# A fused attention, state-space and expert kernel: the order of work in its end phase

## The chip, the core and the metric

The kernel runs on one core of a Trainium2 chip. A core has five engines that each run their own list of instructions in order and wait for each other by semaphores: TensorE (PE in the profile; PEld is its weight load), VectorE (DVE), ScalarE (ACT), GpSimd (POOL) and SyncE (SP), which here issues the loads and stores. The metric is the time of one execution on the device in microseconds (us). Lower is better.

## What is computed

One layer in three parts, for 16 sequences of 128 rows and 512 columns, all in float32:

```python
x = x + xattn(layernorm(x), ctx, ...)   # 16 heads, 2048 context rows a sequence
x = x + mamba_mlp(layernorm(x), ...)
x = x + ffn(layernorm(x), ...)

def mamba_mlp(Z):                       # 1024 channels, 16 states
    x, z = split(Z @ in_proj.T)
    x = silu(causal_conv(x) + conv_b)
    dt, Bm, Cm = split(x @ x_proj.T)    # "B and C projection"
    dt = softplus(dt @ dt_proj.T + dt_b)
    h[t] = exp(dt * A) * h[t-1] + dt * Bm * x   # the scan; y[t] = sum(h * Cm)
    y = ((y + x * D) * silu(z)) @ out_proj.T
    Zm = rmsnorm(y + Z)
    return rmsnorm(gelu(Zm @ w1.T + b1) @ w2.T + b2 + Zm)

def ffn(x):                             # gates from softmax(x @ W_gate), best two
    return x @ W_shared.T + (w1 + w2) * (x @ W_expert.T) + bias
```

The expert routing of the reference has one weight matrix for all experts, and every token keeps both of its places, so its sum is the second matrix times the two gates' sum.

## The kernel before, in words

**Steps.** The whole program is one loop over steps `u` (L1275), written out by hand for all engines. In steps 0 to 255 each step does one head group of the attention for one block of 512 context rows. The state-space part runs behind it: sequences are taken in groups `g` of two, and the 32 scan steps of a group start 54 steps behind its first one (32 for the attention of two sequences and `LAG` = 22). A step does two scans: for each, ACT writes the decays exp(dt A) into a PSUM tile (`decays`, L668), DVE scans over it (`scan`, L683) with inputs that POOL made a step before (`inputs`, L646), multiplies by C and clears the first column again, and POOL adds the product up. `bc` tiles hold B and C spread over all partitions; SP loads them from a small DRAM tensor `bcd`, two steps and one step ahead (`load_bc`, L595).

**Late work.** Tables written ahead of the loop name what else a step does: `late` functions (each with a PSUM bank), `behind`, `middle`, `between`, `after`, `inner` and `loads`. For group g with p = 32(g+1): `x_part` and `z_part` (input projection) in steps p+9 to p+16, `silu_first` a step behind each, `silu_third` on ACT and POOL in the step after that; `x_proj` (L582), the B and C projection, at p+18: 16 matmuls over the eight channel blocks, a DVE copy into the single tile `xd`, a store to `bcd`. `dt_first` (L616) multiplies `xd` again, at p+19 for the first block (L1190), in the table `behind`, which comes after `late` in the step. `projected` (L711), the output projection, follows the last scan of a group: for the last one in steps 311 and 313.

**The end phase.** From step 257 on the attention is over, the last group's scans still run to step 309, and the MLP and expert work of all 16 sequences is fed in. It is cut into pairs `m` of two sequences (0 to 7) and into units (`unit`, L1065): a list of loads, of PE work, and of work behind it (`post`). `feed(k)` (L1102) issues the loads of unit k+2, the extra loads of unit k+1, the post work of unit k-1, then the PE work of unit k. The loop feeds 65 units in 57 steps (L1293), so that eight steps take two; the rest follows behind the loop. For a pair the units are:

- `hidden` 0 to 3 (h0 to h3): 32 matmul instructions each into two banks. Behind each: `gelus`, a load of the GELU table, four GELUs, a load of the table with exp and ln.
- `experts` 0 and 1 (e0, e1), of the pair before: first and second matrix and the gate, 16 + 8 + 16 instructions, one sequence each. Behind them `result`, `gated`, `result_last` and the store of the output.
- `second` 0 to 3 (s0 to s3): 16 instructions each, adding into two banks over all four. Behind s1: `z_norm` of the next pair; s2 ends with `turned_in` of the next pair (transposes), behind it come `turned_pair` (copies to SBUF) and `with_b2`; behind s3: `mlp_sum`.

Of the pair before, `mlp_norm` (behind h0), `last_norm` (behind h1) and `x_turned` (transposes of xf and DVE copies fT, ahead of h3) prepare the experts. The last pair has a unit of its own for `turned_in`, directly behind s3 of pair 6.

**Norm factors.** `inv_sqrt` (L93) has three parts: `root_first`, one DVE add (rv); `root_second`, Ln and Exp on ACT (ry, L83 and L84); `root_third`, a Newton step on DVE (rt and the factor, L89 to L91). `mlp_sum`, `mlp_norm` and `z_norm` call it whole, directly behind the moments.

**Order within a step** (L1275 on): loads, `decays` for the first scan, the feeds, `load_bc` for C, `inputs` of the next step, `silu_third`, the first scan, `decays` for the second, the second scan, `middle`, `late`, `behind`, `after`, `inner`, `silu_second`.

**Banks.** In the end phase six PSUM banks are handed out first in, first out (`bank`, `give_back`, L761): a bank given back in program order may be taken at once, and its next writer then waits for its last reader.

Of the kernel before, what the change touches and what calls it, by code (L numbers as in the profile page):

```python
# [27 lines left out]
MB = 2  # L28
# [6 lines left out]
def perceiver_layer(ctx: ExitStack, tc: tile.TileContext, a: dict, out: bass.AP):  # L35
# [40 lines left out]
    def root_first(pool, src, eps):  # L76
        n = src.shape[1]
        v, y, t = (pool.tile([P, MB], FP, tag=k, name=k)[:, 0:n] for k in ("rv", "ry", "rt"))
        nc.vector.tensor_scalar_add(v, src, eps)
        return v, y, t  # L80

    def root_second(v, y, t):
        nc.scalar.activation(y, v, AF.Ln)  # L83
        nc.scalar.activation(y, y, AF.Exp, scale=-0.5)  # L84

    def root_third(dst, v, y, t):
        for j in range(v.shape[1]):
            dj, vj, yj, tj = (x[:, j : j + 1] for x in (dst, v, y, t))
            nc.vector.tensor_scalar(tj, yj, yj, vj, ALU.mult, ALU.mult)  # L89
            nc.vector.tensor_scalar(tj, tj, -0.5, 1.5, ALU.mult, ALU.add)  # L90
            nc.vector.tensor_scalar(dj, yj, tj, None, ALU.mult)  # L91

    def inv_sqrt(pool, dst, src, eps):  # L93
        r = root_first(pool, src, eps)
        root_second(*r)
        root_third(dst, *r)
# [12 lines left out]
    with ExitStack() as es:  # L109
# [472 lines left out]
        def x_proj(g, ps):  # L582
            ps = ps[:, 0:GT]
            for ec in range(EC):
                nc.tensor.matmul(
                    ps,
                    xproj[:, ec * NX : ec * NX + P],
                    xas[g, ec],
                    start=(ec == 0),
                    stop=(ec == EC - 1),  # L590
                )
            nc.vector.tensor_copy(xd[0:NX, :], ps[0:NX, :])
            nc.sync.dma_start(bcd[g], xd[DTR:NX, :])

        def load_bc(t, base):  # L595

            if 0 <= t < 32 * NG:
                g, q = t // 32, t % 4
                x = ssm.tile([P, NH, GT], FP, tag=f"bc{base}", name=f"bc{t}_{base}")
                rows = bcd[g][base + q * NH : base + (q + 1) * NH, :]  # L600
                nc.sync.dma_start(
                    x.rearrange("p n t -> p (n t)"),
                    rows.rearrange("n t -> (n t)").partition_broadcast(P),
                )
                bcs[t, base] = x
# [348 lines left out]
        def mlp_sum(m, ii):  # L954

            n = len(ii)
            mv2, r, ms = small("mv2", [P, n, 2]), small("r2", [P, n]), small("ms", [P, n])
            for j, i in enumerate(ii):
                x = xrs[m * MB + i]
                nc.vector.tensor_tensor(x, x, accs[m][i], ALU.add)  # L960
                give_back(accs[m][i])
                moments(keep, mv2[:, j, :], x)
            mean_square(keep, ms, mv2)
            inv_sqrt(keep, r, ms, 1e-6)
            stage[m, *ii, "r2"] = r

        def mlp_norm(m, ii):

            n, r = len(ii), stage.pop((m, *ii, "r2"))
            mv3, r3 = small("mv3", [P, n, 2]), small("r3", [P, n])  # L970
            for j, i in enumerate(ii):
                b = m * MB + i
                x = xrs[b]
                nc.vector.scalar_tensor_tensor(
                    x, x, r[:, j : j + 1], fcs["normw"], ALU.mult, ALU.mult
                )
                nc.vector.tensor_tensor(x, x, stage.pop((b, "x1")), ALU.add)
                moments(keep, mv3[:, j, :], x)
            inv_sqrt(keep, r3, mv3[:, :, 1], 1e-5)
            stage[m, *ii, "r3"] = mv3, r3  # L980

        def flat_tile(name):
            return fpool[0].tile([P, D], FP, tag="xf", name=name, bufs=4)

        def last_norm(m, ii):
            mv3, r3 = stage.pop((m, *ii, "r3"))
            for j, i in enumerate(ii):
                b = m * MB + i
                xf = flat_tile(f"xf{b}")
                nc.vector.tensor_scalar(  # L990
                    xf, xrs[b], mv3[:, j, 0:1], r3[:, j : j + 1], ALU.subtract, ALU.mult
                )
                nc.gpsimd.tensor_tensor(xrs[b], xrs[b], fcs["fbias"], ALU.add)
                stage[b, "xf"] = xf

        def gated(m, ii):

# [62 lines left out]

        units = []

        def unit(loads=(), pe=(), post=()):  # L1065
            units.append(([*loads], [*pe], [*post], []))
# [1 line left out]
        def call(f, *xs):  # L1068
            return lambda: f(*xs)

        def turn_unit(m, loads):
            unit(
                loads,
                [call(z_norm, m)] + [lambda i=i, b=b: turned_in(xrs[b], b, "mT") for i, b in seqs(m)],
                [call(turned_pair, m)],
            )

        both = tuple(range(MB))
# [1 line left out]
        def hidden_units(m):  # L1080
            for q in range(0 if m else 2, 4):
                unit([call(load_wf, m, 1, q)], [call(hidden, m, q)], [call(gelus, m, q)])
            if m:
                units[-4][2].append(call(mlp_norm, m - 1, both))
                units[-3][2].append(call(last_norm, m - 1, both))
                units[-1][1].insert(0, call(x_turned, m - 1, both))

        def expert_units(m):
            for i in both:
                unit((), [call(experts, m, both, i)], [call(result, m, i)])  # L1090
            units[-1][2].append(call(gated, m, both))
            units[-1][2].extend(call(result_last, m, i) for i in both)

        def second_units(m):
            for q in range(4):
                unit([call(load_wf, m, 2, q)], [call(second, m, q)])
            units[-4][3].append(call(load_x1, m))
            units[-2][2].append(call(with_b2, m))
            if m < NF - 1:
                units[-1][2].append(call(mlp_sum, m, both))  # L1100

        def feed(k):  # L1102
            for f in (units[k + 2][0] if k + 2 < len(units) else ()):
# [9 lines left out]

        for m in range(NF - 1):
            hidden_units(m)
            if m:
                expert_units(m - 1)
            second_units(m)
            if m < NF - 2:
                units[-4][3].append(call(load_z, m + 1))  # L1120
                units[-3][2].append(call(z_norm, m + 1))
                units[-2][1].extend(
                    lambda i=i, b=b: turned_in(xrs[b], b, "mT") for i, b in seqs(m + 1)
                )
                units[-2][2].append(call(turned_pair, m + 1))
        units[0][0].clear()
        units[1][0].clear()
        feeds = len(units) - 1
# [4 lines left out]
        hidden_units(m)  # L1133
        second_units(m)
        for i in both:
            units[-1][1].extend(call(f, m, (i,)) for f in (mlp_sum, mlp_norm, last_norm))
        expert_units(m - 1)
        units[-1][1].insert(0, call(x_turned, m, (0,)))
        units[-1][1].append(call(x_turned, m, (1,)))
# [11 lines left out]
        def put(where, u, f):  # L1151
            where.setdefault(u, []).append(f)
# [24 lines left out]
        for g in range(NG):  # L1177
            p = 32 * (g + 1)
            for ec in range(EC):
                put(loads, p + 8 + ec, lambda g=g, ec=ec: load_win(g, ec))  # L1180
                put(loads, p + 8 + ec, lambda g=g, ec=ec: load_win(g, EC + ec))
                put(late, p + 9 + ec, lambda ps, g=g, ec=ec: x_part(g, ec, ps))
                put(late, p + 9 + ec, lambda ps, g=g, ec=ec: z_part(g, ec, ps))
                put(after, p + 10 + ec, lambda g=g, ec=ec: silu_first(g, ec, xas))
                put(after, p + Z_GATES[ec], lambda g=g, ec=ec: silu_first(g, ec, zss))
            put(late, p + 18, lambda ps, g=g: x_proj(g, ps))
            s = p + LAG
            for ec in range(EC):
                put(loads, s - 4 + 4 * ec, lambda ec=ec: load_dtproj(ec))
                put(behind, s - 3 + 4 * ec, lambda ps, g=g, ec=ec: dt_first(g, ec, ps))  # L1190
                put(middle, s - 2 + 4 * ec, lambda g=g, ec=ec: dt_second(g, ec))
                put(between, s - 1 + 4 * ec, lambda g=g, ec=ec: dt_third(g, ec))
            for i in range(GB):
                for ec in range(WS):
                    put(loads, s + 32 + 2 * i, lambda g=g, i=i, ec=ec: load_wout(g, i, ec))
                put(loads, s + 31 + 2 * i, lambda b=g * GB + i: reload_x(b))
                put(late, s + 33 + 2 * i, lambda ps, g=g, i=i: projected(g, i, ps))
# [77 lines left out]
        for u in range(last):  # L1275
# [11 lines left out]
                load_ctx(made + 1, ("c01",))  # L1287
            for f in loads.get(u, ()):
                f()
            if scans:  # L1290
                decays(g, r, 0)
            if u > NU:
                while fed < feeds * (u - NU) // (last - 1 - NU):  # L1293
                    feed(fed)
                    fed += 1
            load_bc(u + 1 - 32 - LAG, DS)
            if u == NU + 1:
                load_rows()
# [160 lines left out]
```

## Time and profile before

| what | us |
|---|---|
| median of 3 runs | 3772.5 (3771.56 to 3773.25) |
| the profiled execution | 3772.78 |
| its span, first to last instruction | 3771.0 |

| stretch (us) | PE | DVE | ACT | POOL busy |
|---|---|---|---|---|
| 3094 to 3629: end phase up to the first `projected` of the last group | 514.4 of 535 | 408.0 | 276.2 | 376.8 |
| 3629 to 3771: behind it | 132.4 of 142 | 47.4 | 21.1 | 7.7 |

Matmuls are pipelined, so that a busy PE is not PE at its peak: instructions of 512 columns take 592 ns each in the profile, and 16 of them take 6.9 us. In a line of the waits stand the engine, the tile and line that waited, who released it, the total in us, the times and the longest. In a line of the timeline stand start, length, engine, line, operation, tiles, shape and count; in square brackets the idle time before it and who ended that. "issue" is time for which the profile shows no releaser.

### The profile page before, as it was taken

To read this page: it belongs to the slowest core of one execution; us is meant where nothing else is said; L and a number is where in the kernel's file an instruction comes from. 1 tells how busy PE (TensorE), PEld (TensorE's weight loads), DVE (VectorE), ACT (ScalarE), POOL (GpSimd) and SP (SyncE) were. 2 spreads that over 40 slices of the span, in tenths; PEclk is the share of its full clock that TensorE was granted. 3 is DMA by queue.
4 is the path that set the end of the run, shared out by engine and by line. 5 is a ranking of instruction groups with operands and counts; after the bars stand their busy time and mean duration, and the time that the engine had idled before them with its cause. 6 is when DMAs were issued, how large, how long until landed. Compare 5 with 4: busy or idle time off the path is not lost.

```text
span 3771.0 us, 70359 instructions
## 1 busy us (share of the span) xinstructions
PE 3725.5 (99%) x26120; PEld 2853.4 (76%) x26120; DVE 2705.0 (72%) x4854; ACT 2443.5 (65%) x5848; POOL 2111.2 (56%) x1969
## 2 busy tenths in 40 slices
PE   9999999999999999999999999999999999999999
PEld 7878787778777887788788878787878776655555
DVE  3444445887878777877788778877887777778843
ACT  4555556777767776777677767776777775545431
POOL 2111213675767666766676566766675667677720
PEclk9999999999999999999999999999999999999999
DMA  3111122344444435353534353445344458577742
GB/s 102 35 40 43 51 70 80 132 151 144 144 161 143 155 114 186 130 166 115 187 132 147 125 193 119 155 129 181 137 155 135 163 192 283 188 277 249 266 169 73
DMA packets 343226, 548.42 MB, mean 145 GB/s; under 512 B 24369, under 2 KB 227409, under 8 KB 342625
## 3 DMA queue, kind: packets, MB, share of 16 engines
q1 hardware_dynamic: 342432, 543.27, 43.5%
q8 instruction: 206, 3.38, 0.4%
q14 instruction: 140, 1.14, 0.1%
q0 software_dynamic: 448, 0.63, 0.1%
HBM read 527.29 MB, written 16.52 MB: 144 GB/s over the span
## 4 chain that ended last, share of the span: by engine, by line
PE 91%; DVE 5%; ACT 1%; DMA 1%; issue 1%; POOL 1%; SPq 0%; DVEq 0%; ACTq 0%; POOLq 0%
PE pa L240 24%; PE pc L240 17%; PE bank L333 12%; PE bank L302 7%; PE avp L346 7%; PE bank L531 5%; PE bank L1037 2%; PE bank L942 2%; PE bank L472 2%; PE bank L716 2%; PE bank L911 1%; PE avp L399 1%; PE pc L716 1%; PE pa L942 1%; PE avp L942 1%
## 5 line engine op out<-in xcount | busy, mean ns | idle before, releaser
L310 DVE TENSOR_REDUCE nm<-bank 128x1 f32<-128x512 f32 x1024 | 635.2, 682 | 224.0 <-PE bank L302 223.8
L703 POOL TENSOR_TENSOR ysum<-ysum,w 128x512 f32<-128x512 f32 x384 | 500.3, 1303 | 474.8 <-DVE hst L666 306.8
L320 ACT ACTIVATE pr<-bank,nm 128x512 f32<-128x512 f32 x1024 | 689.8, 687 | 89.9 <-DVE nm L310 84.5
L652 POOL TENSOR_TENSOR w<-dx,bc 128x512 f32<-128x512 f32 x512 | 654.2, 1298 | 8.7
L687 DVE TENSOR_TENSOR_SCAN hst<-hst,w 128x512 f32<-128x512 f32 x459 | 560.7, 1221 | 14.3 <-ACT hst L673 8.1
L338 ACT COPY pT<-bank 128x512 f32<-128x512 f32 x816 | 433.9, 585 | 177.6 <-PE bank L333 173.5
L673 ACT ACTIVATE hst<-dt,alog 128x254 f32<-128x254 f32 x918 | 439.5, 479 | 150.4 <-DVE hst L666 130.7
L333 PE MATMUL bank<-ident,pr 128*128 128x128 f32 x4096 | 507.8, 273 | 3.3 <-ACT pr L320 2.8
L333 PEld LDWEIGHTS bank<-ident,pr 128*128 128x128 f32 x4096 | 467.9, 141 | 47.2 <-issue 11.1
L346 PEld LDWEIGHTS avp<-pT,v 128*32 128x32 f32 x8192 | 208.0, 109 | 193.8 <-issue 176.0
L690 DVE TENSOR_TENSOR w<-hst,bc 128x512 f32<-128x512 f32 x459 | 317.3, 691 | 27.6 <-DMA bc<-bcd 12.0
L232 POOL TENSOR_TENSOR t<-c,c 128x512 f32<-128x512 f32 x128 | 163.2, 1275 | 256.6 <-PE pc L240 252.4
L302 PE MATMUL bank<-kt,qT 32*128 32x512 f32 x2048 | 295.4, 640 | 0.5 <-ACT pT L338 0.5
L346 PE MATMUL avp<-pT,v 128*32 128x128 f32 x8192 | 276.7, 276 | 0.0
L240 PE MATMUL pa<-t,ks 128*128 128x256 f32 x1024 | 248.6, 386 | 0.0
L240 PE MATMUL pa<-vs,t 128*128 128x256 f32 x1008 | 244.7, 386 | 0.0
L240 PEld LDWEIGHTS pa<-vs,t 128*128 128x128 f32 x1008 | 185.4, 190 | 34.6 <-issue 10.1
L240 PEld LDWEIGHTS pa<-t,ks 128*128 128x128 f32 x1024 | 184.8, 190 | 35.2 <-issue 11.6
L320 ACT ACTIVATION_READ_ACCUMULATOR pr<-bank,nm 128x1 f32 x1024 | 210.0, 205 | 0.0
L336 DVE COPY pT<-bank 128x512 f32<-128x512 f32 x208 | 143.8, 691 | 87.5 <-PE bank L333 86.2
L232 POOL TENSOR_TENSOR t<-c,t 128x512 f32<-128x512 f32 x128 | 163.8, 1279 | 36.2 <-issue 19.2
L531 PE MATMUL bank<-zT,win 128*128 128x256 f32 x800 | 183.1, 379 | 0.0
(323 smaller groups left out, 6901.1 us busy)
## 6 DMA issues: line engine op xcount, KB each, us to landing
bc<-bcd SPq DMA_DIRECT2D x512, 512.0 KB, 4.3
c<-in_ctxT_dram SPq DMA_DIRECT2D x256, 256.0 KB, 4.4
wf<-in_w_dram SPq DMA_DIRECT2D x124, 512.0 KB, 6.8
wqo<-in_wqkvo_dram SPq DMA_DIRECT2D x128, 256.0 KB, 4.8
win<-in_win_dram SPq DMA_DIRECT2D x128, 256.0 KB, 4.4
wout<-in_wout_dram SPq DMA_DIRECT2D x128, 256.0 KB, 4.4
x<-in_x_dram SPq DMA_DIRECT2D x16, 256.0 KB, 4.0
x1d<-x SPq DMA_DIRECT2D x16, 256.0 KB, 2.1
```

Of the source, the lines that this page charges most:

```text
L240: nc.tensor.matmul(ps[:, r, :], l[:, kc, r * P : (r + 1) * P], m[:, kc, :], start=(i in (1, 2, 5) and r == 0 and kc == 0), stop=(r == 1 an ...
L302: nc.tensor.matmul(banks[j], qts[b][rows, hg, :], kts[u // 4, hg][rows, :], start=True, stop=True)
L310: nc.vector.tensor_reduce(stats[b][0][j][:, sb, hg : hg + 1], banks[j], AX.X, ALU.max, negate=True)
L320: nc.scalar.activation(pr[:, j, :], banks[j], AF.Exp, bias=nm[j][:, sb, hg : hg + 1], accum_out=sm[:, sb, h : h + 1],)
L333: nc.tensor.transpose(ps[:, j, :], prs[u][:, j, i * P : (i + 1) * P], ident)
L338: nc.scalar.copy(pT, ps)
L346: nc.tensor.matmul(avp[j * HD : (j + 1) * HD, hg, :], vts[u // 4, hg // 2, i // 2][:, i % 2, hg % 2 * P + j * HD : hg % 2 * P + (j + 1) * HD],
L531: nc.tensor.matmul(ps, w[:, kc, :], zTs[g][:, kc, :], start=(kc == 0), stop=(kc == KC - 1))
L652: nc.gpsimd.tensor_tensor(w, dx.unsqueeze(1).to_broadcast([P, NH // 2, GT]), bcs[g * 32 + r, 0][:, i * NH // 2 : (i + 1) * NH // 2, :], AL ...
L673: nc.scalar.activation(bt(h[:, k, :])[:, :, 1:], bt(dt)[:, :, 1:], AF.Exp, scale=aneg[:, ec, n : n + 1],)
L687: nc.vector.tensor_tensor_scan(flat, flat, w.rearrange("p n t -> p (n t)"), 0.0, ALU.mult, ALU.add)
L703: nc.gpsimd.tensor_tensor(s, s, w, ALU.add)
```

## The change

It changes the order alone; every matmul, norm and copy is still done.

- `expert_units(m - 1)` is called behind `second_units(m)` and no longer ahead of it. In the new order a pair's units are h0 to h3, s0 to s3, then e0, e1 of the pair before.
- `x_turned` of the pair before goes from the front of h3 to the front of s2. `fbias` is added in a function of its own, `with_bias`, behind h2; for the last pair it stays directly behind `last_norm`.
- `mlp_sum` and `mlp_norm` only do `root_first`; Ln, Exp and the Newton step are issued at the start of the function that uses the factor, one unit later. `z_norm` is as before.
- `mlp_sum` of pair 6 goes behind `turned_pair` of the last pair's own unit.
- In steps behind 256 the decays of the first scan come behind the feeds.
- `x_proj` of the last group goes from p+18 to p+19 (step 275), the step of its first `dt_first`.

```diff
             mean_square(keep, ms, mv2)
-            inv_sqrt(keep, r, ms, 1e-6)
-            stage[m, *ii, "r2"] = r
+            stage[m, *ii, "r2"] = r, *root_first(keep, ms, 1e-6)
 
         def mlp_norm(m, ii):
-            n, r = len(ii), stage.pop((m, *ii, "r2"))
+            n, (r, *root) = len(ii), stage.pop((m, *ii, "r2"))
+            root_second(*root)
+            root_third(r, *root)
...
-            inv_sqrt(keep, r3, mv3[:, :, 1], 1e-5)
-            stage[m, *ii, "r3"] = mv3, r3
+            stage[m, *ii, "r3"] = mv3, r3, *root_first(keep, mv3[:, :, 1], 1e-5)
...
         def last_norm(m, ii):
-            mv3, r3 = stage.pop((m, *ii, "r3"))
+            mv3, r3, *root = stage.pop((m, *ii, "r3"))
+            root_second(*root)
+            root_third(r3, *root)
...
-                nc.gpsimd.tensor_tensor(xrs[b], xrs[b], fcs["fbias"], ALU.add)
                 stage[b, "xf"] = xf
+
+        def with_bias(m, ii):
+            for i in ii:
+                x = xrs[m * MB + i]
+                nc.gpsimd.tensor_tensor(x, x, fcs["fbias"], ALU.add)
...
-                [call(turned_pair, m)],
+                [call(turned_pair, m), *joins],
...
-                units[-1][1].insert(0, call(x_turned, m - 1, both))
+                units[-2][2].append(call(with_bias, m - 1, both))
...
             units[-4][3].append(call(load_x1, m))
+            if m:
+                units[-2][1].insert(0, call(x_turned, m - 1, both))
             units[-2][2].append(call(with_b2, m))
             if m < NF - 1:
-                units[-1][2].append(call(mlp_sum, m, both))
+                (units[-1][2] if m < NF - 2 else joins).append(call(mlp_sum, m, both))
...
             hidden_units(m)
-            if m:
-                expert_units(m - 1)
             second_units(m)
...
+            if m:
+                expert_units(m - 1)
...
-            put(late, p + 18, lambda ps, g=g: x_proj(g, ps))
+            put(late, p + 18 + (g == NG - 1), lambda ps, g=g: x_proj(g, ps))
...
-            if scans:
+            if scans and u <= NU:
                 decays(g, r, 0)
             if u > NU:
                 while fed < feeds * (u - NU) // (last - 1 - NU):
                     feed(fed)
                     fed += 1
+                if scans:
+                    decays(g, r, 0)
```

More of the change, by code (lines that the diff above doesn't have):

```diff
@@ L1059, in result_last @@
             nc.sync.dma_start(out[b], r)
-        units = []
+        units, joins = [], []
         def unit(loads=(), pe=(), post=()):
@@ L1135, in perceiver_layer @@
         for i in both:
-            units[-1][1].extend(call(f, m, (i,)) for f in (mlp_sum, mlp_norm, last_norm))
+            units[-1][1].extend(
+                call(f, m, (i,)) for f in (mlp_sum, mlp_norm, last_norm, with_bias)
+            )
         expert_units(m - 1)
```

## The prediction

> **What bounds it now.** I read the engine rows of the page first, then TensorE's (PE's) waits between 3080 and 3771 us, where everything lies that the change touches, then the timelines around the long ones.
>
> ```profile
> PE 3725.5 (99%) x26120; PEld 2853.4 (76%) x26120; DVE 2705.0 (72%) x4854; ACT 2443.5 (65%) x5848; POOL 2111.2 (56%) x1969
> ```
>
> PE is never long without work. A shorter kernel can only come from PE's remaining gaps, since the change removes no matmul. The waits of PE in the window:
>
> ```profile
> PE bank L585 <- POOL xa L579: 5.4, 1, 5.4
> PE avp L882 <- DVE xf L990: 4.0, 1, 4.0
> PE bank L911 <- issue: 3.9, 1, 3.9
> PE bank L911 <- DMA wf<-in_w_dram: 3.7, 1, 3.7
> PE bank L882 <- ACT hs L925: 3.2, 1, 3.2
> PE bank L882 <- DVE xr L808: 2.6, 4, 1.0
> PE bank L882 <- DVE xf L990: 1.8, 4, 0.8
> PE bank L911 <- DVE dt L626: 1.2, 1, 1.2
> ```
>
> All waits of that answer add up to 29.9 us. A long wait costs more than its length, because the matmuls behind it run slowly:
>
> ```profile
> 3446.68 1.50 PE L882 MATMUL bank<-ident,xf 128*128 128x128 f32 x8 [3.21 <-ACT hs L925]
> 3447.97 4.93 PE L911 MATMUL bank<-mT,wf 128*128 128x256 f32 x16
> 3452.74 3.62 PE L911 MATMUL pa<-mT,wf 128*128 128x256 f32 x16
> ```
>
> The same 16 matmuls take 4.93 and then 3.62 us; eight transposes take 1.50 instead of 1.04 (3670.27). So this wait costs 3.2 + 1.3 + 0.5 = 5.0 us. The windows view gives a granted clock of 0.72 in 3446 to 3452 and 1.00 in 3610 to 3620. Behind the wait of 1.16 us at 3528.88 the 16 matmuls take 3.72: short waits leave the clock alone. [...]
>
> **The change, part by part.** The unit of PE work: `hidden` and `second` 6.9 us each, an `experts` unit 7.8 (3613.31 to 3621.07), `x_turned` or `turned_in` 0.9.
>
> 1. *Last B and C projection a step on.* It waits 5.44 us for POOL's silu multiply (L579), which ends at 3287.1 while PE stood ready at 3281.5. Slow matmuls behind it add about 2.0 (two L585 in 1.22 against 0.59, two L1037 in 1.92 against 1.02, and the next ones). Moved, it comes behind one more `second` (+6.9) and without `x_turned` in front (-0.9), so its last matmul is due at about 3287.5: the wait goes, **-7.5**. What it issues is 16 matmuls, a DVE copy (0.42) and, in SP's queue, the store to `bcd` (lands in 1.5), now past the step's `load_bc` and weight loads; the loads that read it come a step later (4.3 to land) and their data are used two steps later, some 15 us: covered. New is that `dt_first` now follows in the same step and needs that copy. DVE must first finish the step's two scans; behind the waiting `dt_first` on PE stands the next step's `second`. Bounds: 0.5 (semaphore and copy) to 4 (two scans with their multiplies, 1.22 + 0.69 each, not begun). I take **+1.0**, near the lower end, since DVE was free at 3283.6 and loses the two fT copies of that step.
>
> 2. *Experts behind the next second matrix; x_turned from hidden's last unit to second's third.* The transposes of xf wait 3.2 at 3446 (banks held by late GELUs, **-5.0** with the slow clock) and 4.0 + 0.8 at 3603 (xf late on DVE; the 16 matmuls behind take 4.84 against 3.62 and the transposes 0.5 more: **-6.5**). From `last_norm` to `x_turned` there is now one unit; then there are four, some 28 us of PE work, and from the fT copies to `experts` two instead of one. The remaining xf waits of 1.8 - 0.8 = 1.0 and the 1.2 us for a bank at 3528.88 go too: **-2.2**. What is late next: `turned_in` on `z_norm` (2.6 in all now), which gains 0.9 of cover; and banks. Six banks rotate; I followed them through the new order. In the steady part each is freed a unit or more before it is taken. `load_x1` and `load_z` sit in SP's queue two units nearer to the `mlp_norm` that frees their slots, behind them only bc loads for the next step. The result stores move with `experts` and stand before the same bc load as now.
>
> 3. *Turn unit of the last pair.* Now `mlp_sum` stands in DVE's queue before the copy that `hidden` waits for (PE idle 3.94, then 5.38 for 16 matmuls: 5.7). It moves behind the copy. But the gate and result work of pair 5 now comes before it:
>
> ```profile
> 3393.58 0.69 DVE L1050 TENSOR_TENSOR res<-xr,bank 128x512 f32<-128x512 f32 x1 [5.40 <-PE bank L1037]
> ...
> 3397.20 0.74 DVE L1057 SCALAR_TENSOR_TENSOR res<-pa,gs,res 128x512 f32<-128x512 f32 x1
> ```
>
> That is 4.3 us from the end of `experts`. From the end of `projected`: the sums held by `mlp_sum` leave no spare bank, so `experts` waits 0.95 for DVE's add (0.2 + 0.69), ends at 8.7; 0.2 + 4.3 + copy 0.7 + 0.1 gives 14.0, against 8.6 of work: 5.4 idle in three pieces, the longest 3.4. If that slows the clock as now (1.8), 7.2 against 5.7: **+1.5**; if not, -0.3. I take the former, the piece being longer than 3.21. [...]
>
> 4. *Norm factors a unit later, GELUs ahead of decays.*
>
> ```profile
> ACT ry L83 <- DVE rv L79: 141.9, 24, 27.1
> ACT hst L673 <- DVE hst L666: 58.4, 25, 6.6
> ```
>
> ACT stands behind DVE in both, and GELUs behind ACT. This is what made the bank at 3446 late (3.48 for `ry`, 0.89 for `hst` on ACT just before), so its gain is in part 2. DVE loses 0.51 of wait at each of some 12 roots, off the path. In exchange `mlp_norm` waits for a GELU batch (4.1 us: two table loads of 1.28, four at 0.39), and so do the first decays; behind it on DVE stand the step's scans. DVE's lag is no longer asked for before the next `z_norm`, five units on. `with_bias` only moves two POOL adds (1.4 each) past `last_norm`, to where xf is ready. Cost on PE 0; without that cover, rival B.
>
> For waits that I cannot place (banks, `wout` loads, `z_norm`) I add **+2.0**, between 0 and 8: the trace has 5.8 us of waits under 1.3 each in this window, and PE will run closer to DVE than now.
>
> **Sum:** -7.5 + 1.0 - 5.0 - 6.5 - 2.2 + 1.5 + 2.0 = -16.7. The profiled execution took 3772.8 (span 3771.0), 0.3 above the median shown, so the forecast is 3772.5 - 16.7, about **3756 us**.
>
> **Rivals.**
> - *A, the scan chain caps it.* POOL ends the last gated y at 3618.4 (3617.66 + 0.72); PE reads it in `projected` at 3628.83. Of the 18 us saved before this point only 10.4 can be kept if that chain stays. PE then also has 2.7 us more left to do behind it (two experts and an x_turned for two seconds: 16.5 - 13.8), 1.5 from the turn unit and 1.8 of slow clock: -10.4 + 6.0, **3768**. Against: in 3094 to 3629 DVE is busy 408 of 535 us, and much of the rest is waiting for PE. Chance 0.12.
> - *B, slower: GELUs ahead of decays lengthen that chain.* DVE waits for the second-half decays 12 times, 20.1 us, since a GELU batch lies before them. Now the batch lies before the first half, and each wait grows by one scan, multiply and memset (1.97): +24 on the chain, end 3642. PE waits there: +13.6 + 6.0, **3792**. It decides once the chain ends more than 4.4 us later than now (10.4 - 6.0). For: DVE has little slack behind 3548. Against: where DVE lags, the batch runs in ACT's present wait (58.4). Chance 0.10.
> - *C, the waits only move.* With x_turned relaxed, PE runs on until `z_norm` or a bank, six more times with 1.3 each, 8 in place of 2 and 1.5 of slow clock: **3763**. For: DVE holds at both places today. Chance 0.16, half of it not below 3765.
> - Else the forecast as worked out, 3748 to 3763: 0.62.
>
> The measurement tells some 0.2% (7.5 us) from no change. Faster: 0.62 + 0.08 = 0.70; same: 0.12 + 0.08 = 0.20; slower: 0.10. Range: the lower end has part 1 at +0.5, no unplaced wait, the turn unit at -0.3 and the 2.6 of `z_norm` gone (3749); the upper end takes in A: 3748 to 3770.
>
> **What would show it.** Right: no PE wait at L585, none over 1 us at L882 on xf or GELUs; three pieces of idle at the last turn unit, with slow `hidden` matmuls behind; ACT's wait at L83 down to the seven `z_norm`s and the tail. Wrong: PE waiting at L716 for POOL (A or B), DVE waiting for first-half decays more than 20 us (B), waits at L882 on L808 over 5 us in all (C).

## The result, and the profile after

The changed kernel takes 3762.7 us (median of 8 runs, 3758.7 to 3765.7) against 3771.9 for the kernel before (8 runs): a ratio of 0.9974, 95% interval 0.9964 to 0.9983, or 6 to 14 us less. The forecast was 3756. The profiled execution took 3762.25 us, its span is 3760.5 against 3771.0.

The waits of PE from 3080 to 3761 us in the changed kernel (waiting tile and line, releaser, total, times, longest). Lines have moved: L1037 is now L1043.

```profile
PE bank L911 <- DMA wf<-in_w_dram: 3.7, 1, 3.7
PE pa L911 <- issue: 3.2, 1, 3.2
PE bank L619 <- issue: 2.9, 1, 2.9
PE avp L942 <- DVE dt L626: 2.3, 1, 2.3
PE bank L911 <- issue: 2.2, 1, 2.2
PE avp L716 <- DMA wout<-in_wout_dram: 2.0, 1, 2.0
...
PE bank L882 <- DVE xr L808: 0.7, 2, 0.5
...
PE pa L585 <- POOL xa L579: 0.4, 1, 0.4
```

All waits for xf at L882 are gone, and the one for POOL is down from 5.4 to 0.4. The first line is at the start of the phase and is as before. New are 2.9 at L619 (`dt_first` behind the moved projection), 2.3 at L942 and 2.2 at L911 (banks), and 2.0 instead of 1.0 for a load of `wout`. What came new behind the projection (first fence) and in the turn unit (second fence) is seen on PE's timeline:

```profile
3288.10 0.70 PE L585 MATMUL pa<-xa,xproj 128*128 128x256 f32 x2 [0.41 <-POOL xa L579]
3291.67 0.67 PE L619 MATMUL bank<-xd,dtw 128*128 128x256 f32 x2 [2.87 <-issue]
3292.18 8.73 PE L942 MATMUL bank<-wf,hs 128*128 128x512 f32 x16
```

```profile
3651.19 1.12 PE L1043 MATMUL avp<-wex,fT 128*128 128x512 f32 x2 [0.78 <-DVE xn L725]
...
3660.07 1.09 PE L882 MATMUL bank<-ident,xn 128*128 128x128 f32 x8 [0.85 <-DVE res L1056]
3664.38 5.38 PE L911 MATMUL pa<-mT,wf 128*128 128x256 f32 x16 [3.22 <-issue]
```

The 16 instructions behind `dt_first` take 8.73 instead of 7.03 us: the granted clock is 0.81 from 3291 to 3300 us, which costs 1.7 us. In the turn unit stand the three pieces of idle that were forecast, with 5.38 against 3.62 us behind them.

### The profile page after: what moved, and what is told of

It is laid out like the page before. It is cut to its first block, busy times and chain, and to the rows that moved or that the text cites. A ratio compares the mean times of both kernels' runs of the same rounds, so it can differ in the third digit from the quotient of the medians.

```text
span 3760.5 us, 70389 instructions
## 1 busy us (share of the span) xinstructions
PE 3722.9 (99%) x26120; PEld 2851.7 (76%) x26120; DVE 2706.2 (72%) x4854; ACT 2446.9 (65%) x5848; POOL 2112.4 (56%) x1969
## 4 chain that ended last, share of the span: by engine, by line
PE 94%; DVE 2%; DMA 1%; ACT 1%; issue 1%; POOL 0%; SPq 0%; DVEq 0%; ACTq 0%; POOLq 0%
PE pa L240 24%; PE pc L240 17%; PE bank L333 12%; PE bank L302 7%; PE avp L346 7%; PE bank L531 5%; PE bank L942 4%; PE bank L911 2%; PE bank L1043 2%; PE bank L472 2%; PE avp L399 1%; PE bank L716 1%; PE pc L716 1%; PE avp L942 1%; PE pa L911 1%; PE pc L531 1%
```

## The experiments

Twelve kernels were run, each in five rounds beside the kernel before. The kernel before had medians of 3772.5 to 3774.1 us there, so the ratios are compared; 0.001 is 3.8 us. "Change" in the table says which parts a kernel has: O the order of units with `x_turned`, `with_bias` and the last `mlp_sum`; X the moved projection; R the norm factors a unit later; G the GELUs ahead of the first decays.

| kernel | change | ratio to before (95% interval) | about, us |
|---|---|---|---|
| the changed kernel | O X R G | 0.9974 (0.9964 to 0.9983) | -10 |
| e1 | X | 0.9988 (0.9980 to 0.9997) | -5 |
| e2 | O | 0.9974 (0.9963 to 0.9984) | -10 |
| e3 | R | 1.0032 (1.0019 to 1.0044) | +12 |
| e4 | G | 1.0009 (1.0000 to 1.0017) | +3 |
| e5 | O X R | 1.0004 (0.9995 to 1.0013) | +2 |
| e6 | O X G | 0.9991 (0.9983 to 1.0000) | -3 |
| e7 | O R G | 0.9981 (0.9972 to 0.9989) | -7 |
| e10 | O X | 0.9966 (0.9954 to 0.9979) | -13 |
| e8 | O X R G, copies on ACT | 0.9966 (0.9954 to 0.9979) | -13 |
| e9 | O X R G, `dt_first` a step later | 0.9974 (0.9965 to 0.9984) | -10 |
| e11 | O X R G, turn unit repaired | 0.9955 (0.9942 to 0.9967) | -17 |
| e12 | O X, turn unit repaired | 0.9955 (0.9942 to 0.9969) | -17 |

### One part alone on the kernel before

**e1, the projection.** The edit on the kernel before (e1, e3 and e4 also have `with_bias` as a function of its own, called directly behind `last_norm`, where the adds stood):

```diff
-            put(late, p + 18, lambda ps, g=g: x_proj(g, ps))
+            put(late, p + 18 + (g == NG - 1), lambda ps, g=g: x_proj(g, ps))
```

> The kernel before, with only the last B and C projection a step on. My theory, from the trace of the changed kernel: the wait of 5.4 us for POOL goes with its 2.0 us of slow clock (-7.5), and the new wait of dt_first for the copy of xd comes (2.9 us of wait and 1.3 of slow clock): about -3 us, 3769. Rival: the move only exchanges one wait for another of the same price: no change, 3772.

Measured -5 us. The wait for POOL is gone, and the new wait of `dt_first` is shorter here than in the changed kernel, with no slow clock behind it: the first two instructions of 512 columns take 1.02 us, the usual time.

```profile
3291.76 0.67 PE L619 MATMUL avp<-xd,dtw 128*128 128x256 f32 x2 [1.68 <-issue]
```

So the exchange of waits pays. The interval takes in the -3 that was expected.

**e2, the order.** The kernel before, with the diff's lines on `expert_units`, `x_turned`, `with_bias` and `joins`:

> The kernel before, with only the new order of units: experts behind the next pair's second matrix, x_turned three units later, fbias in its own function, the last mlp_sum behind the copies. My theory: both long waits of the transposes of xf go (-11.5), the small ones (-2.2), the turn unit costs 1.5 more: about -12 us, 3760, and the wait for POOL at the B and C projection stays. Rival: the late GELUs and norm factors are the cause, and the waits only move to the banks: -3 us at most, 3769.

Measured -10 us: as much as the whole change. The waits of its PE (3080 to 3771 us):

```profile
PE bank L585 <- POOL xa L579: 5.4, 1, 5.4
PE bank L911 <- DMA wf<-in_w_dram: 3.8, 1, 3.8
PE avp L911 <- issue: 3.2, 1, 3.2
PE bank L882 <- DVE xr L808: 2.8, 3, 1.9
PE bank L716 <- DMA wout<-in_wout_dram: 2.0, 1, 2.0
PE bank L942 <- DVE dt L626: 1.9, 1, 1.9
```

No wait for xf is left, though ACT stands behind DVE's moments and the decays as before. The wait for POOL is there as before, and so are the new ones for `wout`, for the bank that `dt_first` held, and in the turn unit. So these three come with the order, not with the ACT parts (the norm factors a unit later and the GELUs ahead of the decays).

**e3, the norm factors, and e4, the GELUs.** The kernel before, with the diff's lines on `root_first`, `root_second` and `root_third` (e3), or with its last two hunks alone (e4):

> The kernel before, with only the norm factors of mlp_sum and mlp_norm made one unit later. My theory: in the old order x_turned comes one unit behind last_norm, and last_norm now waits on ACT for a GELU batch; so xf comes later and PE waits longer: 0 to +8 us, 3772 to 3780. Rival: ACT is freed of its waits for the moments, the banks come free earlier and the wait at 3446 us goes: -5 us, 3767.

> The kernel before, with only the GELUs ahead of the first scan's decays. My theory: the wait for a bank at 3446 us shrinks, but the scans start later and the wait for xf on DVE at 3603 us grows: within 4 us of the kernel before, 3768 to 3774. Rival: GELUs behind decays are the main cause of PE's waits: -7 us or more, 3765.

e3 is slower by 12 us, more than expected, and e4 by 3, with an interval that starts at no change. DVE's largest wait from 3094 to 3620 us in e3, and PE's waits for xf there:

```profile
DVE rt L89 <- ACT ry L84: 34.4, 18, 4.7
```

```profile
PE bank L882 <- DVE xf L992: 12.1, 4, 7.9
PE avp L882 <- DVE xf L992: 7.9, 1, 7.9
```

In the kernel before DVE waited 9.1 us at L89 in this stretch, 0.5 each time. Now Ln and Exp stand on ACT behind a GELU batch, which stands behind decays, which wait for the scan that DVE has yet to do (ACT waits 99.9 us there, against 56.1 in the kernel before). xf comes later, and PE waits for it. A further wait of 6.2 us at L882 ends with ACT's `sg` (L568). In e4 the wait for late GELUs at 3446 us has become one for xf, so that PE waits 7.8 us for xf in all against 5.8 before, and 4.7 instead of 1.2 for banks that `dt_first` holds.

### One part out of the changed kernel

**e5, e6 and e7.** The changed kernel, with decays ahead of the feeds again (e5), `inv_sqrt` called whole behind the moments again (e6), or the projection back at p+18 (e7):

```diff
-            if scans and u <= NU:
+            if scans:
                 decays(g, r, 0)
...
-                if scans:
-                    decays(g, r, 0)
```

> The changed kernel, with the first scan's decays ahead of the feeds again. My theory: with x_turned moved PE no longer needs the GELUs early, and DVE's waits for first-half decays (28.9 us in the changed kernel) go: 0 to -4 us against the changed kernel, 3759 to 3763. Rival: the GELUs ahead of the decays carry a share of the gain: 3767 or more.

> The changed kernel, with whole norm factors directly behind the moments again. My theory: mlp_norm no longer waits for a GELU batch, so the wait of 2.2 us at 3270 us goes: about -2 us against the changed kernel, 3760. Rival: ACT stands behind DVE's moments again and GELUs come late: +4 us, 3767.

> The changed kernel, with the last B and C projection at its old step. My theory: the wait for POOL's multiply comes back with its slow clock (+7.5) and the wait of dt_first goes (-4.2): about +3 us, 3766. Rival: the earlier GELUs have already taken that wait away, so that only the wait of dt_first goes: -4 us, 3758.

e7 came as expected: 2.6 us lost against the changed kernel, which the intervals do not tell from none; in its trace PE waits 7.06 us for POOL at L585 and no longer for the copy at L619. e5 and e6 went the rivals' way: 11 and 6 us lost (the intervals of e6 and of the changed kernel just meet, at 0.9983). But this does not show that the two ACT parts bring the gain, because each one does harm without the other (e3, e4). Waits of the kernels with one of them, from 3094 to 3620 us, ACT's and DVE's, two of e5 and then two of e6:

```profile
ACT hst L673 <- DVE hst L666: 106.2, 30, 8.0
```

```profile
DVE rt L89 <- ACT ry L84: 34.0, 18, 4.7
```

```profile
ACT ry L83 <- DVE rv L79: 116.7, 18, 13.0
```

```profile
DVE hst L687 <- ACT hst L673: 41.0, 15, 6.8
```

With late norm factors alone (e5) the Ln and Exp stand behind decays that wait for DVE. With early GELUs alone (e6) the decays stand behind Ln and Exp that wait for DVE's moments, and the scans behind the decays. On PE the price shows as longer waits at L619 (4.7 and 4.6 us against 2.9 in the changed kernel) and for `z_norm` at L882 (3.9 and 5.9 against 0.7), in e5 also as 4.4 for GELUs at L911. With both parts, in the changed kernel, neither engine waits for so long:

```profile
DVE hst L687 <- ACT hst L673: 28.9, 15, 5.2
...
DVE rt L89 <- ACT ry L84: 8.5, 10, 3.9
```

**e10, both ACT parts out** (the edits of e5 and e6 together):

> The kernel before, with the new order of units and the last B and C projection a step on, without the norm factors a unit later and without the GELUs ahead of the decays. If the parts add up as run alone (about -10 and -5 us): -14 us, ratio 0.9963, and the two ACT parts are worth nothing beside them. Rival: the two ACT parts, taken together, belong to the gain of the new order, as each of them taken out alone cost 8 to 12 us: ratio 0.999 or more.

Measured -13 us, about the sum of e1 and e2 (-14). In the new order the two ACT parts undo each other's harm and bring nothing measurable: the change's -10 and e10's -13 lie within each other's intervals. The first expectation holds; its rival, which I had drawn from e5 and e6, falls. Both parts together on the old order were not run.

### What is left in the changed kernel

**e9, `dt_first` behind the next feed:**

```diff
-                put(behind, s - 3 + 4 * ec, lambda ps, g=g, ec=ec: dt_first(g, ec, ps))
+                if g == NG - 1 and ec == 0:
+                    put(early, s - 2, dt_early)
+                else:
+                    put(behind, s - 3 + 4 * ec, lambda ps, g=g, ec=ec: dt_first(g, ec, ps))
```

> The changed kernel, with the first dt_first of the last group issued behind the feed of step 276 and no longer in step 275 right behind the projection whose copy it needs. My theory: the wait of 2.9 us and the slow clock behind it (1.3 us) go, and the six later steps of dt have slack: -4 us against the changed kernel, ratio to the kernel before 0.996 to 0.997. Rival: dt then comes late for the inputs of step 277 and the scan chain passes the delay on: no gain, 0.9975.

No gain; the rival was right in its outcome. PE no longer waits for the copy at L619, but DVE, in order, now waits 4.9 us for dt, and the `z_norm` behind it comes late for the transposes:

```profile
3308.71 1.11 PE L882 MATMUL pa<-ident,xr 128*128 128x128 f32 x4 [3.23 <-DVE xr L808]
3310.39 1.11 PE L882 MATMUL bank<-ident,xr 128*128 128x128 f32 x4 [0.56 <-DVE xr L808]
```

**e8, the copies of the last pair on ACT:**

```diff
-                copy = nc.vector.tensor_copy if i else nc.scalar.copy
+                copy = nc.vector.tensor_copy if i and m < NF - 1 else nc.scalar.copy
```

> The changed kernel, with both copies of the last pair's turned z on ACT, which is idle there, so that hidden no longer waits for DVE's gate and result work. My theory: the last piece of idle shrinks from 3.2 to about 0.8 us and the slow clock behind it (1.8 us) goes: -4 us against the changed kernel, 3758.5. Rival: the slow clock comes from all three pieces of idle together and stays: -2.4 us, 3760.

The time fell by 3 us, which the intervals do not tell from none, and the trace does not bear my theory out. The last piece shrinks only to 1.97, since `hidden` then waits for a bank that `result_last` still holds, and the slow clock does not go, as the rival had it:

```profile
3657.44 1.09 PE L882 MATMUL bank<-ident,xn 128*128 128x128 f32 x8 [0.85 <-DVE res L1056]
3660.50 6.73 PE L911 MATMUL pa<-mT,wf 128*128 128x256 f32 x16 [1.97 <-issue]
```

The 16 matmuls take 6.73 us, still longer than the 5.38 of the changed kernel. Start of these to start of the next 16 is 6.56 against 5.22, so what the shorter wait gained (1.25) is lost again in this trace. The 2.6 us by which the span is shorter than the changed kernel's therefore lie outside the turn unit, where the edit changes nothing.

**e11, the turn unit repaired.** `mlp_sum` of pair 6 goes back behind s3, and of pair 5 the gate and result work goes behind the copies:

```diff
-                (units[-1][2] if m < NF - 2 else joins).append(call(mlp_sum, m, both))
+                units[-1][2].append(call(mlp_sum, m, both))
...
-            units[-1][2].append(call(gated, m, both))
-            units[-1][2].extend(call(result_last, m, i) for i in both)
+            behind_last = joins if m == NF - 3 else units[-1][2]
+            behind_last.append(call(gated, m, both))
+            behind_last.extend(call(result_last, m, i) for i in both)
```

> The changed kernel, with mlp_sum of pair 6 at its usual place behind its last second unit, and the gate and result work of pair 5 behind the copies of the last pair's turned z. My theory: the banks of the sums come free early, so the three pieces of idle (0.8, 0.9, 3.2 us) become one of about 1 us, and the slow clock behind them (1.8 us) goes: -5.5 us against the changed kernel, ratio to the kernel before 0.996. Rival: mlp_sum now stands in DVE's queue ahead of the projection's add, and the first piece grows: no gain, 0.9975.

Measured -17 us against the kernel before, 7 better than the changed kernel by the ratios, whose intervals overlap a little, and 5.9 by the spans. One short piece of idle is left in the turn unit, and no slow clock, which is 5.8 us less than the changed kernel's 4.85 idle and 1.76 slow:

```profile
3660.14 3.69 PE L911 MATMUL bank<-mT,wf 128*128 128x256 f32 x16 [0.83 <-ACT mT L903]
```

**e12, the same repair without the ACT parts** (e10 and e11 together):

> The kernel before, with the new order of units, the last B and C projection a step on, and the repaired turn unit (mlp_sum of pair 6 at its usual place, the gate and result work of pair 5 behind the copies), without the two ACT parts. My theory: the repair takes some 6 us here as well, so -18 us against the kernel before, ratio 0.9952, and the two ACT parts are not needed for the best version. Rival: with the ACT parts missing, the repair meets a DVE that is later, and the ratio stays at 0.996 or above.

Measured -17 us, 3756.6, as e11. Against e10 that is 4 us by the ratios, whose intervals overlap; in the trace the turn unit is as in e11, with one piece of 0.83 and the 16 matmuls in 3.69. So the repair works with and without the ACT parts. These two are the fastest versions of the study.

## Why the prediction was right, and where it was off

The sign, the place and the mechanism were right: PE's long waits set the time, the order takes those for xf (e2), the step on takes the one for POOL (e1). The size was off, -10 measured against -16.7. That the measured time is the figure of rival C, 3763, is chance: by its sign C did not come (see below). The terms in the profile (with the slow clock behind a wait):

| term | forecast | measured | from |
|---|---|---|---|
| projection: wait for POOL | -7.5 | -7.1 | 0.41 left (the 2.0 of slow clock is the forecast's; from start to start the trace of before has 1.6) |
| new wait of `dt_first` | +1.0 | +4.6 | 2.87, and 8.73 - 7.03 |
| waits for xf at 3446 and 3603 | -11.5 | -11.5 | none left |
| small ones (xf, bank at 3528) | -2.2 | -2.2 | none left |
| turn unit | +1.5 | +0.9 | 4.85 idle and 1.76, against 5.7 |
| not placed: banks, `wout`, `z_norm` | +2.0 | +5.1 | 2.20 + 2.35; `wout` 1.0 more and 1.5 slow (4 matmuls in 3.46 against 1.98); `z_norm` 0.7 against 2.6 |
| sum | -16.7 | -10.2 | spans: -10.5 |

- **Two terms failed by size:** the wait of `dt_first`, and what I could not place. For the first I named both scans of the step as the upper end (4) and took 1.0, since DVE had been free at 3283.6. In the changed kernel it was free at 3283.2 too, but the scan could not start before 3287.09:

```profile
3287.09 1.23 DVE L687 TENSOR_TENSOR_SCAN hst<-hst,w 128x512 f32<-128x512 f32 x1 [3.30 <-ACT hst L673]
...
3291.16 0.41 DVE L592 COPY xd<-pa 64x256 f32<-64x256 f32 x1
```

  It waited for decays behind a GELU batch on ACT. I had counted that exchange as free on PE. e10 has no GELUs ahead of the first decays, and its PE waits 3.57 at the same place: there the batch stands ahead of the second scan's decays, for which DVE waits 1.90. So the early GELUs alone are not the cause; with either order a scan of this step waits behind the batch. On the kernel before (e1) the wait was 1.68, not far from my figure. The slow clock that I left out at +1.0 is the other half of the miss.
- **"Cost on PE 0" for the ACT parts** held for the pair (e10 against the change), but as a balance: e10 waits 3.8 us for `z_norm` at L882 where the changed kernel waits 0.7, and the changed kernel waits 4.55 for banks (2.20 + 2.35) where e10 waits 1.6. I had not worked this balance out, so the 0 was in part luck. That they must come as a pair I did not see: alone they cost 12 and 3 us in the old order, and with the other one missing 11 and 6 in the new. One cost of the pair can be read: the wait of 2.20 us at 3270.66 ends with a DVE read of a bank that came 3.87 us late because `mlp_norm` waited for ACT, and it is absent in e2, e6 and e10, which have no late norm factors.
- **The slow clock in the turn unit** came as I took it, here and in the six other kernels with the same three pieces of idle (e2, e5, e6, e7, e9, e10). But the reason that I gave, a piece longer than 3.21, does not hold by itself. In e4 a wait of 3.24 was followed by 16 matmuls in the usual 3.62:

```profile
3448.51 1.08 PE L882 MATMUL bank<-ident,xf 128*128 128x128 f32 x8 [3.24 <-DVE xf L990]
3449.43 3.62 PE L911 MATMUL bank<-mT,wf 128*128 128x256 f32 x16
```

- **"Its gain is in part 2"** was right in that the order takes the wait at 3446 without any help from ACT (e2).
- **Banks.** I had followed them and found each "freed a unit or more before it is taken". One that `dt_first` holds at 291 is taken at 292, where two feeds fall into one step, and DVE was then late: 2.35 us in the change, 1.9 in e2.
- **Rival A** did not come: PE does not wait for POOL at L716. **Rival B** has its mechanism in the trace, and its sign too: DVE's waits for first-half decays rose from under 4 to 28.9 us, over the 20 that I had named. Its price did not come. The 20.1 us of waits for second-half decays went in exchange, which B left out, so that both together rose by some 8 us only, and PE did not wait for the end of the chain. **Rival C** describes part of the miss, two bank waits, but not its own sign: the waits at L882 on L808 are 0.7 us and not over 5. ACT's wait at L83 fell, from 73.9 to 37.2 us between 3094 and 3620, but came 11 times there and not only at the `z_norm`s.

## What to carry to other kernels

When one engine is the bound and nearly always busy, list its few long waits, price each with the slow matmuls that may follow it, as a range, and give the waiting step another unit of distance: here that was all of the gain. Before moving work to "behind", look at what else goes to the same place: the turn unit lost its `mlp_sum` and got the gate work instead, and the repair was worth some 6 us more in the traces. Parts that tie two in-order queues together must be tested in pairs: taking one out of the finished kernel showed a loss, and yet both together bring nothing measurable.

## What the runs showed of the hardware

- In these traces it does not follow from the length of a wait whether the matmuls behind it run slowly. The same two waits, first in the changed kernel and then in e8:

```profile
3270.66 3.69 PE L911 MATMUL bank<-mT,wf 128*128 128x256 f32 x16 [2.20 <-issue]
...
3360.78 3.46 PE L716 MATMUL avp<-wout,zs 128*128 128x512 f32 x4 [1.99 <-DMA wout<-in_wout_dram]
```

```profile
3269.87 5.38 PE L911 MATMUL bank<-mT,wf 128*128 128x256 f32 x16 [2.19 <-issue]
...
3359.84 1.98 PE L716 MATMUL avp<-wout,zs 128*128 128x512 f32 x4 [1.81 <-DMA wout<-in_wout_dram]
```

  The first wait left the pace in the changed kernel (also in e7, e9 and e11, 3.69 each), but not in e8, where the granted clock was 0.68 from 3269.8 to 3275.1; with the second it is the other way round. Of the waits over 1.1 us that stood alone, one of 1.86 us in e5 has slow matmuls behind it (16 in 5.41), while behind the 3.24 of e4 nothing ran slowly. Behind the same three pieces of the turn unit, 0.78, 0.85 and 3.2, the 16 matmuls took 5.12 us in e6, 5.38 in the changed kernel and 6.73 in e5; behind the single 0.83 of e11 they took 3.69. The edit of e8 lies in the turn unit, some 300 us behind the second of the two waits shown. So two kernels can differ by 1.5 or 1.7 us behind one wait where nothing ahead of it was edited. What decides it was not shown.
- The runs of the changed kernel spread over 7 us, those of the kernel before beside them over 2. The four runs at a granted clock of 0.998 took 3758.7 to 3762.5 us, the three at 0.997 took 3762.9 to 3764.2, the one at 0.996 took 3765.7. In the runs of the kernel before the order is not so strict: beside e9 to e11 it took 3773.0 at 0.998 and 3771.6 at 0.996. What sets the clock of a run was not tried.
